# The order of 32 node tiles in two eight-head graph attention layers: from few edges to many, or few and many in turn

## The chip, the cores and the metric

The kernel runs on one core of one Trainium2 chip. The metric is the device time of one execution in microseconds (us), as a median of several runs.

## What is computed

The reference takes 4096 nodes with 512 features each (x) and a sparse 0/1 matrix adj. The chance of an edge between nodes i and j falls as 1/sqrt((i+1)(j+1)), so node 0 has many neighbours and node 4095 few. It runs two blocks, cut here to what matters:

```python
# block 0: eight heads of 64
h = einsum('nf,kfp->knp', x, W)
e = leaky_relu(f2[:, :, None] + f1[:, None, :])        # one score for each pair and head
att = softmax(where(adj > 0, e, -1e16), axis=-1)
x = layernorm(x + concat_heads(einsum('knm,kmp->knp', att, h)))
# block 1: eight heads of 64, then one head of 512, then two dense layers
h = elu(gat_heads(x, mask, W1, a1))
out = elu(gat_heads(h, mask, Wo, ao))
out = relu(out @ lin1_w + lin1_b) @ lin2_w + lin2_b
x = layernorm(x + out)
```

## The kernel before

The nodes are cut into 32 tiles of 128, tile 0 with the first 128 nodes. A first stage, `find_edges`, reads adj and writes a list of edges for each tile, in chunks of 128 edges: for each edge of a chunk the neighbour's number (`idx`) and the node's place in the tile (`nl`). How many chunks a tile has is fixed when the program is built, by the statistics of adj: 51 for tile 0, 21 for tile 1, 16, 14 and 13 for tiles 2 to 4, 11 for 5 and 6, 10 for 7, 9 for 8 to 10, 8 for 11 to 13, 7 for 14 to 19, 6 for 20 to 28 and 5 for 29 to 31. That is 309 chunks. `units_of` (line 1049) joins the chunks of a tile to units of at most 6: 11 units for tile 0, 4 for tile 1, 3 each for 2 to 4, 2 each for 5 to 19 and 1 each for 20 to 31. That is 66 units.

The two eight-head layers are two calls of `heads_layer` (line 1270); a third layer with one head and the dense layers follows and is written out below it with an order of its own. Each layer works from a table in HBM, one row for each node (its projected features and its score as a neighbour), and one row more, the mean of all, for nodes without edges. The first gather of a layer waits until the whole table of that layer stands.

What a layer does with a unit, in the class `Attention`:

- `gather` (line 1076): one indirect DMA for each chunk, issued by POOL, brings 128 rows of the table to a buffer g. The pool has `GB` = 7 buffers, each for one unit; the gather of unit i + 7 is issued after unit i and waits until PE has done with unit i's buffer.
- `spread` (lines 1094 to 1129), once for a tile: PE spreads the nodes' own scores to the edges (pss, lines 1101 and 1108), in cuts of at most 20 chunks; DVE collects each cut (line 1117) and makes ls (1129). There is one pss buffer. Where a tile has more than one cut, all but the last are collected at once, in the middle of DVE's queue.
- `weights` (1147 to 1155): DVE makes z of three small operations, ACT takes two exponentials, one of them (wp) to a single PSUM buffer.
- `add` (1179 to 1212): DVE makes the 0/1 matrices sm (1179) and multiplies the gathered rows by wp (1200); PE sums them over the edges into acc (1212), which has two buffers, each for one tile.

The order of all this is written out by hand in `heads_layer`. Its list `order` is 31, 30, ... 0, few edges first. Before the loop stand the gathers of the first 7 units, the spreads of the first two tiles and the weights of the first unit. One turn of the loop, for unit i, is: at a tile's first unit the spread of the tile two places on and the fetch of its input rows; `project`; the weights of unit i + 1; `add` of unit i; the gather of unit i + 7; then `split`, `rows`, `norm`, and at a tile's first unit `divide` for the tile before. So in DVE's queue z of the next unit stands ahead of the multiply of this one. These five steps finish a tile, one step a turn: `divide` (1220, 1232, then residual and layer norm statistics in the first layer, 1393 to 1259, or the elu in the second, 1247 and 1248), `norm` (1263 to 1266, or 1249, then a transpose on PE, 683, copied out by ACT, 686), `project` (697, into the next layer's features), `rows` (710 to 717, ACT copies them and SP writes them to the next layer's table), and `split` (723 to 733). A spread needs the result of `split` for its tile. It is made for 8 tiles at once, when the last of them is there; in the order 31 to 0 that is the tile that 8 divides.

After the last unit the mean row is finished (768 to 770) and written. In the first layer ACT clears the 7 buffers with one operation each before they are first used.

Of the kernel before, what the change touches and what calls it, by code (L numbers as in the profile page):

```python
# [24 lines left out]
NT = N // P  # L25
# [533 lines left out]
def sparse_path(  # L559
# [119 lines left out]
    def turn_in(sb, ps, st, src, t):  # L679

        pt = ps.tile([P, FC, P], F32, name="pt", tag="ph")
        for c in range(FC):
            nc.tensor.transpose(pt[:, c, :], src[:, ts(c, P)], ident)  # L683
        xt = sb.tile([P, FC, P], F32, name="xt")
        for c in range(FC):
            nc.scalar.activation(  # L686
                xt[:, c, :], pt[:, c, :], AF.Copy, accum_out=st.xparts[:, c, t : t + 1]
            )
        return xt

    def project_in(ps, st, columns, n=P):

        halves = []
        for j in range(2):
            ph = ps.tile([P, st.wide], F32, name="ph")
            for c in range(FC):
                nc.tensor.matmul(ph[:n], columns(c), st.w[:, c, j], start=(c == 0), stop=(c == FC - 1))  # L697
            halves.append(ph)
        return halves

    def project_out(sb, st, halves, t, n=P):

        hs = st.heads
        hrow = sb.tile([P, F + HS], F32, name="hrow")[:n, : st.row]
        if hs == 1:
            nc.scalar.copy(hrow[:, 0:1], ones[:n])
        for j, ph in enumerate(halves):
            part = HF + hs // 2 if hs > 1 else HF + j
            at = j * st.part if hs > 1 else 1 + j * HF
            nc.scalar.copy(hrow[:, at : at + part], ph[:n, :part])  # L710
        nc.sync.dma_start(st.table[t * P : t * P + n, :], hrow)
        st.hrow = hrow
        if t < NT:
            for j, ph in enumerate(halves):
                m = hs // 2 if hs > 1 else 1 - j
                if m:
                    nc.scalar.copy(st.s[:, t, j * m : (j + 1) * m], ph[:, st.wide - m :])

    def split_s(sb, st, lo, n):

        shape = [P, n, 2, st.heads]
        s2 = sb.tile([P, 8, 2, HS], F32, name="s2")[:, :n, :, : st.heads]
        nc.vector.tensor_tensor(
            s2,
            st.s[:, lo : lo + n, None, :].to_broadcast(shape),
            half[:, None, :, None].to_broadcast(shape),
            op=OP.mult,
        )
        part = st.s3[:, lo : lo + n]
        nc.vector.tensor_copy(part[:, :, :, 0, :], s2)  # L730
        nc.vector.tensor_sub(s2, s2, part[:, :, :, 0, :])
        nc.vector.tensor_copy(part[:, :, :, 1, :], s2)
        nc.vector.tensor_sub(part[:, :, :, 2, :], s2, part[:, :, :, 1, :])
# [8 lines left out]
    def mean_of_all_but(pool, ps, st, t):  # L742

        rest = pool.tile([P, 2, FC], F32, name="rest_mean")
        for i, (lo, hi) in enumerate(((0, t), (t + 1, NT))):
            if lo < hi:
                nc.vector.tensor_reduce(rest[:, i], st.xparts[:, :, lo:hi], AX.X, OP.add)
            else:
                nc.vector.memset(rest[:, i], 0.0)
        nc.vector.tensor_add(rest[:, 0], rest[:, 0], rest[:, 1])  # L750
        nc.vector.tensor_scalar_mul(rest[:, 0], rest[:, 0], 1.0 / N)
        halves = project_in(ps, st, lambda c: rest[:, 0, c : c + 1], 1)
        mrow = pool.tile([1, F + HS], F32, name="mrow")[:, : st.row]
        if st.heads == 1:
            nc.scalar.copy(mrow[:, 0:1], ones[:1])
        for j, ph in enumerate(halves):
            part = HF + st.heads // 2 if st.heads > 1 else HF + j
            at = j * st.part if st.heads > 1 else 1 + j * HF
            nc.scalar.copy(mrow[:, at : at + part], ph[:1, :part])
        return mrow  # L760
# [288 lines left out]
    def units_of(order):  # L1049
        units = []  # L1050
        for t in order:
            own = [
                Unit(t, [(p.first + i, n) for i, n in runs], slots)
                for p in pts if p.t == t for runs, *slots in p.units()
            ]
            own[0].first = own[-1].last = True
            units += own
        return units
# [211 lines left out]
    def heads_layer(gp, wk, sb, pp, st, nxt, fetch, finish, clear):  # L1270

        order = list(range(NT - 1, -1, -1))
        units = units_of(order)
        with tc.tile_pool(name=f"ha_{st.name}", bufs=2, space=PSUM, reuse_waits="tile") as pacc, \
                tc.tile_pool(name=f"hp_{st.name}", bufs=1, space=PSUM, reuse_waits="tile") as one, \
                tc.tile_pool(name=f"hq_{st.name}", bufs=2, space=PSUM, reuse_waits="tile") as ps, \
                tc.manual_schedule():  # L1280
            at = Attention(st, gp, wk, pacc, one)
            extra = {}
            if clear:
                for _ in range(GB):
                    g = gp.tile([P, GC * (F + HS)], F32, name="g")
                    nc.scalar.activation(g, ones.to_broadcast(g.shape), AF.Copy, scale=0.0)
            for u in units[:GB]:
                at.gather(u)
            for t in order[:2]:
                at.spread(t)()  # L1290
                extra[t] = fetch(t)
            at.weights(units[0])

            def divide(t):
                at.inverse(sb, t)
                o = at.normal(sb, t)
                return norm, t, o, finish(o, t, extra.pop(t))

            def norm(t, o, rest):
                rest()
                xt = turn_in(pp, ps, nxt, o, t)
                return project, t, xt

            def project(t, xt):
                return rows, t, project_in(ps, nxt, lambda c: xt[:, c, :])

            def rows(t, halves):
                project_out(pp, nxt, halves, t)  # L1310
                return (split, t) if t % 8 == 0 else None

            def split(t):
                split_s(pp, nxt, t, 8)

            def run(of):
                for way in list(ways):
                    if way[0] is of:
                        ways.remove(way)
                        nxt_ = of(*way[1:])  # L1320
                        if nxt_:
                            ways.append(nxt_)

            ways = []
            for i, u in enumerate(units):
                pos = order.index(u.t)
                spread = None
                if u.first and pos + 2 < NT:
                    spread = at.spread(order[pos + 2])
                    extra[order[pos + 2]] = fetch(order[pos + 2])  # L1330
                run(project)
                if i + 1 < len(units):
                    at.weights(units[i + 1])
                if i == len(units) - 1:
                    mrow = mean_of_all_but(pp, ps, nxt, u.t)
                at.add(u)
                if i + GB < len(units):
                    at.gather(units[i + GB])
                run(split)
                run(rows)  # L1340
                run(norm)
                if u.first and pos > 0:
                    ways.append((divide, order[pos - 1]))
                    run(divide)
                if spread:
                    spread()
            ways.append((divide, order[-1]))
            while ways:
                for of in (project, split, rows, norm, divide):
                    run(of)  # L1350
            finish_mean(ps, nxt, mrow)
# [4 lines left out]
    with ExitStack() as pools:  # L1356
# [6 lines left out]
        pp = pools.enter_context(tc.tile_pool(name="eq", bufs=2, space=PSUM))  # L1363
# [20 lines left out]
    pp = layers.enter_context(tc.tile_pool(name="lp", bufs=2, side="right", reuse_waits="tile"))  # L1384
# [7 lines left out]
    def finish0(o, t, xr):  # L1392
# [7 lines left out]
        return rest  # L1400

    heads_layer(gp, wk, sb, pp, st0, st1, fetch0, finish0, True)
    heads_layer(gp, wk, sb, pp, st1, st2, lambda t: None, lambda o, t, _: elu(sb, o), False)


    layers.close()
    with tc.tile_pool(name="tg", bufs=GT, side="right", reuse_waits="tile") as gp, \
# [12 lines left out]
        order = [t for block in blocks for t in block]  # L1420
# [176 lines left out]
```

## Time and profile before

| | us |
|---|---|
| median of 3 runs | 2143.87 (2143.78 to 2149.99) |
| the profiled execution's own time | 2328.89 |
| its span, first to last instruction | 2326.7 |
| first gather of the two eight-head layers and of the one-head layer | 499.7, 1031.7, 1556.5 |
| last L1200 multiply of the two eight-head layers ends | 1006.5, 1527.3 |
| mean granted TensorE clock | 0.885 of full |

| engine | busy us | share of the span |
|---|---|---|
| PE (matrix products) | 1776.6 | 76% |
| DVE (vector engine) | 1328.1 | 57% |
| POOL (issues the gathers) | 1161.8 | 50% |
| ACT (scalar engine) | 658.9 | 28% |

The profiled execution is 185.0 us longer than the median run, and 2.2 us of it lie around its span. A line of the timeline has start and duration in us, the engine, the line of the program, the operation, what it writes and reads, how many of it, and in brackets how long its engine was idle before it and what ended the idle time. A line of waits has the waiting operation, what it waited for, the total in us, how many times, and the longest. A line of a stretch has its bounds, its length, the busy time of PE, PE's weight loads, DVE, ACT and POOL with the number of instructions, the granted clock, the busy share of the DMA engines, and GB/s.

### The profile page before, as it was taken

Reading aid. Unit: us, or ns where it says so; the run is one execution under the profiler, and the core shown is the slowest. Engines: PE = TensorE matmul, PEld = TensorE weight load, DVE = VectorE, ACT = ScalarE, POOL = GpSimd, SP = SyncE. Lnnn points to the kernel's source line nnn. Section 1 sums busy time; section 2 is a strip of 40 time slices with the busy share of each in tenths; the row PEclk is TensorE's granted clock in tenths of the full one; section 3 lists DMA queues with packets and bytes.
Section 4 is the critical chain, followed back from the end, with each engine's and each line's share of the span. In section 5 each row is a group of like instructions: output and inputs, shape, how many; then the busy total and the mean of one; then the engine's idle time right before and its main releaser. Section 6 shows DMA issues by size and latency. Waiting matters only on the chain.

```text
span 2326.7 us, 29282 instructions
## 1 busy us (share of the span) xinstructions
PE 1776.6 (76%) x8987; PEld 1038.4 (45%) x8987; DVE 1328.1 (57%) x3920; ACT 658.9 (28%) x2311; POOL 1161.8 (50%) x1662
## 2 busy tenths in 40 slices
PE   4778776643987775754997767746999898998997
PEld 3555442212665543531665444424445444444444
DVE  6887776744998776733777655733243424334322
ACT  3446776650332211100433221101111111121121
POOL 5424444456556664627556665646355634444300
PEclk9989997866999896875999988877999999999999
DMA  6434665525667775625566665545354524335301
GB/s 222 141 115 159 224 256 207 210 80 163 201 209 219 212 209 144 174 60 145 154 159 170 175 182 145 158 128 143 87 150 131 170 81 148 101 110 151 93 16 52
DMA packets 132589, 351.94 MB, mean 151 GB/s; under 512 B 41922, under 2 KB 42954, under 8 KB 128454
## 3 DMA queue, kind: packets, MB, share of 16 engines
q0 software_dynamic: 74160, 206.25, 33.1%
q1 hardware_dynamic: 58262, 143.72, 17.5%
q8 instruction: 74, 1.21, 0.2%
q14 instruction: 93, 0.76, 0.1%
HBM read 347.31 MB, written 42.24 MB: 167 GB/s over the span
## 4 chain that ended last, share of the span: by engine, by line
PE 36%; DVE 12%; issue 9%; another core or an unknown queue 6%; DMA 3%; POOL 3%; ACT 2%; SPq 0%; DVEq 0%; POOLq 0%; ACTq 0%
PE acc L1212 13%; PE p L1475 9%; PE ph L697 6%; PE p L1487 5%; DVE g L1200 4%; POOL g L1076 3%; DMA g<-table_t,idx 2%; DMA xr<-sx_d 1%; PE pt L683 1%; DVE bs L1253 1%; DVE sm L1179 1%; DVE sm L1187 1%; DVE xr L1492 1%; DVE z L1147 1%
## 5 line engine op out<-in xcount | busy, mean ns | idle before, releaser
L1076 POOL DMA_INDIRECT g<-table_t,idx x927 | 937.4, 1011 | 720.1 <-PE acc L1212 352.9
L1212 PE MATMUL acc<-g,sm 128*64 128x260 f32 (+2 forms) x4068 | 619.9, 424 | 219.9 <-DVE g L1200 100.7
L1212 PEld LDWEIGHTS acc<-g,sm 128*64 128x64 f32 x4068 | 347.9, 150 | 462.7 <-issue 177.8
L697 PE MATMUL ph<-sw_t,xt 128*128 128x264 f32 (+1 forms) x1536 | 408.4, 415 | 82.1 <-ACT xt L686 46.3
L697 PEld LDWEIGHTS ph<-sw_t,xt 128*128 128x128 f32 x1536 | 303.4, 204 | 154.2 <-ACT xt L686 63.0
L1200 DVE TENSOR_TENSOR g<-g,wp 128x2048 f32<-128x2048 f32 (+3 forms) x132 | 349.1, 2645 | 22.8 <-ACT wp L1155 20.2
L884 DVE MAX8 cand<-key 128x8 f32<-128x353 f32 (+55 forms) x467 | 197.3, 449 | 77.7 <-PE key L878 77.1
L1475 PE MATMUL p<-sht,sl1w 128*128 128x512 f32 (+1 forms) x576 | 229.3, 553 | 2.2 <-issue 1.2
L1487 PE MATMUL p<-sl2w,shid 128*128 128x512 f32 x512 | 227.0, 598 | 0.0
L686 ACT ACTIVATE xt<-pt 128x128 f32<-128x128 f32 x384 | 101.1, 278 | 286.5 <-PE pt L683 132.3
L710 ACT COPY hrow<-ph 128x260 f32<-128x260 f32 (+2 forms) x194 | 71.1, 373 | 311.1 <-PE ph L697 146.2
L1475 PEld LDWEIGHTS p<-sht,sl1w 128*128 128x128 f32 x576 | 107.6, 191 | 114.0 <-issue 108.7
L1487 PEld LDWEIGHTS p<-sl2w,shid 128*128 128x128 f32 x512 | 95.4, 190 | 120.1 <-issue 119.3
L1249 DVE SCALAR_TENSOR_TENSOR o<-ex,o 128x512 f32<-128x512 f32 x64 | 44.4, 694 | 182.8 <-ACT ex L1248 145.1
L877 PE MATMUL key<-sg,s_identb 128*128 128x512 bf16 (+1 forms) x258 | 111.6, 434 | 15.4 <-DVE cand L884 10.1
L848 ACT ACTIVATE sg<-raw 128x4096 bf16<-128x4096 int32 (+1 forms) x39 | 116.9, 2998 | 6.6 <-DMA raw<-in_adj_dram 3.7
L1478 ACT ACTIVATE shid<-p,sl1b 128x512 f32<-128x512 f32 (+1 forms) x72 | 46.0, 639 | 249.5 <-PE p L1475 212.0
L878 PE MATMUL key<-frac,places 128*128 128x512 bf16 (+1 forms) x258 | 111.1, 431 | 2.7 <-POOL places L784 2.7
L1187 DVE TENSOR_SCALAR sm<-iota_n,nl,w 128x64 f32<-128x64 f32 x339 | 83.1, 328 | 31.9 <-ACT w L1158 31.1
L1147 DVE TENSOR_TENSOR z<-s,g 128x16 f32<-128x16 f32 (+9 forms) x291 | 43.6, 174 | 92.0 <-DMA g<-table_t,idx 83.7
L1117 DVE TENSOR_REDUCE s<-pss 128x48 f32<-128x144 f32 (+21 forms) x108 | 32.1, 298 | 102.3 <-remote 55.1
L686 ACT ACTIVATION_READ_ACCUMULATOR xt<-pt 128x1 f32 x384 | 79.7, 208 | 0.0
(185 smaller groups left out, 1811.3 us busy)
## 6 DMA issues: line engine op xcount, KB each, us to landing
raw<-in_adj_dram SPq DMA_DIRECT2D x31, 2048.0 KB
table_t<-hrow SPq DMA_DIRECT2D x64, 260.0 KB
xr<-in_x_dram SPq DMA_DIRECT2D x64, 256.0 KB
g<-table_t,idx POOLq DMA_INDIRECT x927
table_t<-hrow SPq DMA_DIRECT2D x32, 257.0 KB
sx_d<-o SPq DMA_DIRECT2D x32, 256.0 KB
xr<-sx_d SPq DMA_DIRECT2D x32, 256.0 KB
out_dram<-xr SPq DMA_DIRECT2D x32, 256.0 KB
```

Source lines behind the costliest of these rows:

```text
L686: nc.scalar.activation(xt[:, c, :], pt[:, c, :], AF.Copy, accum_out=st.xparts[:, c, t : t + 1])
L697: nc.tensor.matmul(ph[:n], columns(c), st.w[:, c, j], start=(c == 0), stop=(c == FC - 1))
L848: nc.scalar.activation(sg[:, ts(i, w)], raw[:, ts(i, w)], AF.Sign)
L877: nc.tensor.matmul(out_, ident_b, sg[:, j:e], start=True, stop=False)
L878: nc.tensor.matmul(out_, places[:, w], frac[:, j - w * KW : e - w * KW], start=False, stop=True)
L884: nc.vector.max(out=cand[:, at : at + 8], in_=part)
L1076: nc.gpsimd.indirect_dma_start(out=u.g[:, k, : self.st.row], out_offset=None, in_=self.st.table[:, :], in_offset=bass.IndirectOffsetOnAxis ...
L1187: nc.vector.tensor_scalar(sm[:, at + i], of_g, node[k], u.w[:, k], op0=OP.is_equal, op1=OP.mult)
L1200: nc.vector.tensor_mul(body, body, wp[:, :, :, None].to_broadcast(body.shape))
L1212: nc.tensor.matmul(out_[g * HN : (g + 1) * HN], sm[:, slot], rows(k), start=start, stop=stop)
L1475: nc.tensor.matmul(p1, l1w[:, c, ts(k, P)], hts[b][:, c, :n], start=(c == 0), stop=(c == FC - 1))
L1487: nc.tensor.matmul(p2, hids[b][:, k, ts(j, P)], l2w[:, k, :], start=(k == 0), stop=(k == HC - 1))
```

## The change

The list `order` is made anew in both eight-head layers: 31, 1, 30, 15, 29, 2, 28, 14, 27, 3, 26, 13, 25, 4, 24, 12, 23, 5, 22, 11, 21, 6, 20, 10, 19, 7, 18, 9, 17, 8, 16, 0. Tile 31 is still first and tile 0 last. Because groups of 8 tiles no longer end with the tile that 8 divides, `rows` keeps a set of the tiles that are out, and calls for the split of a group when all 8 are in it. Nothing else differs; the third layer keeps its order.

```diff
-        order = list(range(NT - 1, -1, -1))
+        many = [t for i in range(8) for t in (1 + i, NT // 2 - 1 - i)][: NT // 2 - 1]
+        order = [t for pair in zip(range(NT - 1, NT // 2, -1), many) for t in pair] + [NT // 2, 0]
+        assert sorted(order) == list(range(NT))
...
             def rows(t, halves):
                 project_out(pp, nxt, halves, t)
-                return (split, t) if t % 8 == 0 else None
-
-            def split(t):
-                split_s(pp, nxt, t, 8)
+                out_.add(t)
+                lo = t // 8 * 8
+                return (split, lo) if out_.issuperset(range(lo, lo + 8)) else None
+
+            def split(lo):
+                split_s(pp, nxt, lo, 8)
...
-            ways = []
+            ways, out_ = [], set()
```

## The prediction

> **What bounds the kernel now.** I read the page first, then the waits of each engine, then the timeline by tile. I call the two eight-head layers A (first gather at 499.7 us) and B (1031.7 us); the one-head layer's gathers begin at 1556.5 us. One layer gathers 309 chunks (927 over three layers) in 66 units (132 L1200 multiplies in A and B).
>
> ```profile
> L1076 POOL DMA_INDIRECT g<-table_t,idx x927 | 937.4, 1011 | 720.1 <-PE acc L1212 352.9
> ```
>
> The page's costliest group is the gather on POOL: 937.4 us of work, and 720.1 us of idle before it, half of that for a buffer which PE's acc has yet to free. So it is both the largest job and one that is often held up. The timeline at the start of B gives POOL's pitch and when a unit can be used:
>
> ```profile
> 1031.74 1.00 POOL L1076 DMA_INDIRECT g<-table_t,idx  x1 [39.65 <-DMA table_t<-mrow]
> 1033.04 0.99 POOL L1076 DMA_INDIRECT g<-table_t,idx  x1 [0.30 <-issue]
> ...
> 1036.95 1.00 POOL L1076 DMA_INDIRECT g<-table_t,idx  x1 [0.30 <-issue]
> ...
> 1040.59 0.20 DVE L1147 TENSOR_TENSOR z<-s,g 128x40 f32<-128x40 f32 x1 [10.86 <-DMA g<-table_t,idx]
> ```
>
> One gather every 1.30 us, so 309 x 1.304 = 402.9 us a layer if POOL never stands. The fifth chunk is issued by 1037.95 and DVE starts on it at 1040.59: 2.6 us to land.
>
> Next, stretches of the layers (us, then busy PE, PEld, DVE, ACT, POOL). Counting L1200 multiplies, the first line is tiles 24 to 20 of A, the second tiles 18 to 15, the third tile 0; then tiles 24 to 20 and tile 0 of B.
>
> ```profile
> 601.00:644.40 43.40, 41.21 (x268) 29.28 (x266) 41.12 (x89) 13.71 (x80) 20.08 (x20) 1.00 0.66 191
> 659.90:701.00 41.10, 34.28 (x231) 23.22 (x229) 38.28 (x100) 11.82 (x70) 26.91 (x26) 1.00 0.74 223
> 951.30:1006.50 55.20, 45.63 (x262) 27.84 (x260) 43.44 (x89) 7.03 (x39) 28.23 (x29) 0.88 0.46 128
> ```
> ```profile
> 1129.60:1169.70 40.10, 38.28 (x258) 27.71 (x259) 32.20 (x59) 17.25 (x85) 19.05 (x19) 1.00 0.50 138
> 1469.90:1527.30 57.40, 46.09 (x264) 28.13 (x263) 41.30 (x82) 8.14 (x40) 32.68 (x31) 0.91 0.47 127
> ```
>
> In A a tile of 6 chunks takes 43.40 / 5 = 8.68 us with DVE full, against 6 x 1.304 = 7.8 us of POOL: the consumers are behind. Tile 0 takes DVE 43.4 us of work against 51 x 1.304 = 66.5 us of POOL: POOL is behind, and lives on up to 7 units gathered ahead. In B the same tiles take 8.02 us (PE full) and 41.3 us of DVE. So the two regimes are real.
>
> Is time lost by their order? That needs a correction: the profiled execution is 2328.89 us against the median of 2143.87, 185.0 us more. PE's waits in A (first fence) and B (second) say where:
>
> ```profile
> PE acc L1212 <- issue: 27.8, 25, 2.9
> PE pss L1101 <- issue: 14.0, 2, 13.3
> PE ph L697 <- issue: 7.1, 11, 1.6
> ```
> ```profile
> PE acc L1212 <- issue: 43.7, 44, 7.0
> PE ph L697 <- issue: 22.9, 11, 13.6
> PE pss L1101 <- issue: 7.7, 2, 4.9
> ```
>
> "issue" is idle time for which the profile shows no cause; at 1068 to 1090 us PE starts single matmuls about 0.7 us apart. Sums: A 50.4 us with 1.5 of pss L1108, plus 21.3 of DVE "rd L1220 <- remote" at tiles 29 and 28; B 82.0 with pt L683 (5.7) and pss L1108 (2.0); the rest of the program 28.1. Together 181.8, close to 185.0: I take them as the tracing's own (an inference) and leave them out.
>
> A then lasts 1031.7 - 499.7 - 71.7 = 460.3 us, B 1556.5 - 1031.7 - 82.0 = 442.8. POOL's floor is 402.9, plus 6.6 from the last gather to the end of the last multiply (2.6 landing, 1.1 of z and exp, 2.8 multiply), plus the tail to the next layer's first gather (25.2 in A from 1006.5, 29.2 in B from 1527.3): 434.7 and 438.7. **A is 25.6 us over the floor, B 4.1.** That is all that an order can win: 29.7 us.
>
> [...]
>
> **The change part by part.** Instructions of every engine stay the same in number and size; POOL's 309 gathers per layer change only in which chunk they fetch. Only order moves.
>
> (1) Spread of tile 1 (21 chunks, two cuts, so DVE waits for PE in the middle of its queue) goes from tile 3's first unit to before the layer's first unit. In A DVE stood from 859.83 until PE's record ends at 865.7: 5.9 us removed. At the new place it is hidden under the wait for the first gather: in B the split of tiles 0 to 7, on which it now depends, ends at 1029.1 us and its two collects (0.66 and 0.17 us) have until 1040.6. If that cover were gone it would cost about 2 us. Spread of tile 0 (four cuts) goes from tile 2 to tile 8: same cost at either place, 0.
>
> (2) Tile 1 comes second, when POOL has no lead. A unit's multiply stands behind the next unit's z (L1147) in DVE's queue, so tile 1's last multiply needs 31 gathers: 31 x 1.304 + 2.6 + 1.1 + 1.8 = 45.9 us after the first gather. Unstarved it would be there at 16.8 (first multiply, 516.5 - 499.7) + 2.8 + 20.1 (tile 1's 25.9 us of period less 5.8 of idle) = 39.7: starved 6.2. Before, the first tiles starve 2.1 (DVE z <- DMA g). Cost 4.1 us. Queued behind that z on DVE are the multiply, norm and divide; nobody else waits long. Tile 1's own idle of 5.8 us lies inside the starved time, of which I count 3.5 (the wait of rd for PE) as gained.
>
> (3) POOL's lead before tile 0. By then DVE in A has done the pairs 31,1 to 17,8 and 16; POOL too, at nearly equal sums (pair 30,15: 8.68 + 41.10 / 4 = 19.0 against 12 x 1.304 = 15.6 us; pair 29,2: 8.68 + 18.3, tile 2's period less its idle, = 27.0 against 21 x 1.304 = 27.4). Lead at tile 0 is some units, as before. 0; bounds: A falls to its floor (-25.6), or the pairs leave A where it is.
>
> (4) SP: fetches, table and sx_d writes go with their tiles, same count. The layer's last row written is still tile 0's and then the mean, so the next layer's first gather waits for the same thing. 0. Splits of three groups come late (tiles 16, 8, 0) instead of spread: 5 small DVE operations each, 1.5 us, moved only.
>
> Sum for A: -5.9 + 4.1 - 3.5 = -5.3. For B, where POOL is within 4.1 us of being the bound, the same edits can give between 0 and -4.1; I take -1. Total -6: 2143.9 - 6 = **2138 us** (profiled about 2323). That is 0.27%, and 0.3% (6.4 us) is about what a measurement of this kernel can tell from no change.
>
> **Rivals.** *Full interleave:* with every pair near balance, A and B both end on POOL's floor: 2143.9 - 29.7 = 2114. For it: DVE's busy time from 516 to 1007 us is 366 us, under POOL's 403. Against: A's other 52 us (460.3 - 25.2 - 16.8 - 366) are waits inside units, which the order hardly touches.
>
> *Exposed finishing (slower):* the finishing of a tile runs through ACT and is hidden only in long units. In A and B:
>
> ```profile
> DVE rstd L1263 <- ACT rstd L1259: 21.6, 10, 5.3
> ```
> ```profile
> DVE o L1249 <- ACT ex L1248: 33.3, 14, 6.0
> ```
>
> But for 4.4 us at tile 26, A's part is in the 16 tiles 19 to 4, of two and three short units; tiles 25 to 20 show 0.2 us of idle each. Alternated, the 12 single-unit tiles are finished inside short units too. With the smaller rows of L1263, 26.4 - 4.4 = 22.0 us over 16 tiles is 1.4 us each; 12 more tiles cost 16.5 us in A, and B is covered by POOL. Then 2138 + 16.5 = 2154. It decides if these waits are real and not the echo of PE's unexplained waits, and if A's consumers, not POOL, end last; above 6 us it ends slower.
>
> *Nothing moves:* (1) and (2) cancel and POOL's blocked time was all tracing: 2144.
>
> **How the numbers follow.** Forecast 0.40 (2130 to 2144), full interleave 0.17, exposed finishing 0.25, nothing 0.18. Faster: half of the forecast and the interleave, 0.37. Same: half the forecast, most of the last, a little of the third, 0.37. Slower: 0.26. Range 2120 to 2158: it cuts the lower half of the interleave and the upper tail of the exposed finishing. The forecast's own range is 2130 to 2144.
>
> **What would show it.** In the changed profile: (1) no wait of some 20 us at L1117 in mid-layer; (2) waits of L1147 for g at tile 1's units, some 6 us a layer; (3) POOL's wait for acc in A far below 69.8 us if the interleave holds; the rival shows as L1263 and L1249 waiting on ACT more often than 10 and 14 times. I am wrong if PE's unexplained waits are real work, since then both layers are bound by the consumers throughout, or if a split or spread at a new place stops PE.

## The result and the profile after

| kernel | us, median | runs | ratio to before, 95% interval |
|---|---|---|---|
| before | 2143.82 (2140.20 to 2149.99) | 8 | |
| after | 2136.68 (2131.30 to 2139.29) | 8 | 0.9974 [0.9964, 0.9985] |

The change makes the kernel 0.26% faster, 5.6 us by the ratio, near the forecast of 2138. (The medians differ by 7.1 us; the recorded ratio lies closer to 1, and gains are taken from it here unless medians are named.) The number came out. Most of the steps that led to it did not, as the rest shows.

The first profile of before (2328.89 us) was taken where PE was slowed far more than in the runs of after in this table (granted clock 0.885, against 0.914 to 0.921), so I compare the profile of after (0.918) with a second profile of before (2146.02 us, 0.915, called *before again*).

The line that answers to the first one of the prediction, from the page of after:

```profile
L1076 POOL DMA_INDIRECT g<-table_t,idx x927 | 937.8, 1012 | 535.9 <-issue 229.1
```

The gathers cost POOL the same 1.01 us each, but the idle time before them fell from 720.1 to 535.9 us, and a buffer that PE has yet to free is no longer what ends most of it. The timeline at the start of B, in after:

```profile
944.12 1.00 POOL L1076 DMA_INDIRECT g<-table_t,idx  x1 [36.00 <-DVE ls L1129]
945.42 0.99 POOL L1076 DMA_INDIRECT g<-table_t,idx  x1 [0.30 <-issue]
...
949.32 1.00 POOL L1076 DMA_INDIRECT g<-table_t,idx  x1 [0.30 <-issue]
...
953.15 0.20 DVE L1147 TENSOR_TENSOR z<-s,g 128x40 f32<-128x40 f32 x1 [9.64 <-DMA g<-table_t,idx]
```

The pitch is 1.30 us, as before, and the first unit is usable 2.8 us after its last gather was issued. The release that is named for the first gather is a DVE operation, which ended at 943.51 us. But the gather starts 0.86 us after a DMA that landed at 943.26, and in before again, where the mean row's write (table_t) is the release named, it also starts 0.86 us after the landing (952.45 after 951.59); so I take that write to be what it waits for here too.

Whole layers, A then B: first for before again, then for after (columns as in the prediction: bounds, length, PE, PEld, DVE, ACT, POOL, clock, DMA share, GB/s).

```profile
505.05:952.45 447.40, 348.80 (x2234) 230.33 (x2234) 370.91 (x840) 116.37 (x588) 313.04 (x309) 0.91 0.71 210
952.45:1395.44 442.99, 344.13 (x2235) 229.55 (x2235) 313.55 (x648) 123.34 (x583) 324.64 (x314) 0.90 0.67 186
```
```profile
500.50:944.10 443.60, 353.81 (x2234) 232.60 (x2234) 372.52 (x840) 116.83 (x588) 313.69 (x309) 0.90 0.71 212
944.10:1384.10 440.00, 342.81 (x2224) 227.27 (x2224) 313.91 (x647) 123.65 (x583) 321.71 (x313) 0.92 0.69 188
```

Read the second column. A went from 447.4 to 443.6, B from 443.0 to 440.0, with the same work on every engine. POOL is "busy" for 313 us only, since the 0.30 us between two gathers are not counted; from its first gather to the end of its last it is 408 us. So a layer is best cut into three pieces that follow one another: POOL's gathers (with the time in which POOL is *held up*, that is, its idle over 0.30 us before a gather, counted where it is over 0.6), the *lag* from the end of the last gather to the end of the last multiply, and the *tail* from there to the next layer's first gather. The waits of POOL in A show what changed, before again and then after (waiting operation, what for, total us, times, longest):

```profile
POOL g L1076 <- PE acc L1212: 8.8, 7, 2.4
```
```profile
POOL g L1076 <- PE acc L1212: 1.2, 4, 0.3
```

Before, POOL stood in A seven times for a buffer, 8.8 us, of which 7 x 0.30 are the usual pause; after, the four waits are nothing but usual pauses. In the timeline of before again, five waits are longer than 0.6 us. Four of them, 5.0 of the 6.4 us beyond the usual pauses, lie at tiles 15 to 13, just after tiles 31 to 16; the second, in tile 15, is the first pair of lines here. The fifth lies in tile 0, near the end of A, in the second pair:

```profile
639.46 1.00 POOL L1076 DMA_INDIRECT g<-table_t,idx  x1 [0.30 <-issue]
642.33 0.99 POOL L1076 DMA_INDIRECT g<-table_t,idx  x1 [1.87 <-PE acc L1212]
...
904.65 1.00 POOL L1076 DMA_INDIRECT g<-table_t,idx  x1 [0.30 <-issue]
907.42 1.00 POOL L1076 DMA_INDIRECT g<-table_t,idx  x1 [1.78 <-PE acc L1212]
```

### The profile page after: what moved, and what is told of

Read it like the earlier page. It is cut to its first block, busy times and chain, and to the rows that moved or that the text cites. A ratio compares the mean times of both kernels' runs of the same rounds, so it can differ in the third digit from the quotient of the medians.

```text
span 2136.3 us, 29277 instructions
## 1 busy us (share of the span) xinstructions
PE 1721.8 (81%) x8987; PEld 1004.8 (47%) x8987; DVE 1328.6 (62%) x3920; ACT 663.4 (31%) x2311; POOL 1162.0 (54%) x1662
## 4 chain that ended last, share of the span: by engine, by line
PE 33%; DVE 17%; issue 16%; POOL 15%; DMA 12%; ACT 6%; SPq 0%; POOLq 0%; DVEq 0%; ACTq 0%
POOL g L1076 10%; DMA g<-table_t,idx 10%; PE acc L1212 10%; PE p L1479 9%; PE ph L697 6%; DVE g L1200 4%; PE p L1491 4%; DVE cand L884 2%; POOL s L944 1%; ACT sides L943 1%; DMA xr<-sx_d 1%; DVE cand L901 1%; DVE sm L1179 1%; DVE lst L899 1%; PE pl L967 1%
## 5 line engine op out<-in xcount | busy, mean ns | idle before, releaser
L1076 POOL DMA_INDIRECT g<-table_t,idx x927 | 937.8, 1012 | 535.9 <-issue 229.1
L1212 PE MATMUL acc<-g,sm 128*64 128x260 f32 (+2 forms) x4068 | 581.0, 416 | 182.7 <-DVE g L1200 141.6
L1212 PEld LDWEIGHTS acc<-g,sm 128*64 128x64 f32 x4068 | 327.9, 148 | 402.1 <-DVE g L1200 159.5
L697 PE MATMUL ph<-sw_t,xt 128*128 128x264 f32 (+1 forms) x1536 | 399.5, 409 | 54.3 <-ACT xt L686 47.8
L697 PEld LDWEIGHTS ph<-sw_t,xt 128*128 128x128 f32 x1536 | 296.5, 199 | 126.3 <-ACT xt L686 70.6
L1147 DVE TENSOR_TENSOR z<-s,g 128x16 f32<-128x16 f32 (+8 forms) x291 | 46.6, 175 | 162.7 <-DMA g<-table_t,idx 161.6
L1249 DVE SCALAR_TENSOR_TENSOR o<-ex,o 128x512 f32<-128x512 f32 x64 | 44.2, 691 | 122.0 <-ACT ex L1248 121.8
L1155 ACT ACTIVATE wp<-z 128x32 f32<-128x32 f32 (+3 forms) x132 | 27.2, 206 | 211.2 <-DVE g L1200 211.2
L1496 DVE TENSOR_TENSOR xr<-p,xr 128x512 f32<-128x512 f32 x32 | 22.0, 689 | 93.6 <-PE p L1491 93.2
```

Of the source, the lines that this page charges most:

```text
L1076: nc.gpsimd.indirect_dma_start(out=u.g[:, k, : self.st.row], out_offset=None, in_=self.st.table[:, :], in_offset=bass.IndirectOffsetOnAxis ...
L1212: nc.tensor.matmul(out_[g * HN : (g + 1) * HN], sm[:, slot], rows(k), start=start, stop=stop)
```

## The experiments

Times of a group are set beside before's runs on the same chip: 2141.04 us (e1 to e4), 2140.95 (e5 to e8), 2317.62 (e9 to e11) and 2142.01 (e12). The pieces of each profile are in this table, in us; the profile of before again is e1. "Rest" is from the third layer's first gather to the end of the last DVE operation (L1266), some 6 us before the span ends.

| run | order in A | A: gathers (held up) + lag + tail | A | order in B | B: gathers (held up) + lag + tail | B | rest |
|---|---|---|---|---|---|---|---|
| e1 | old | 413.8 (6.4) + 10.8 + 22.8 | 447.4 | old | 407.8 (0) + 8.4 + 26.8 | 443.0 | 742.3 |
| after | new | 407.6 (0) + 12.8 + 23.2 | 443.6 | new | 404.9 (0) + 8.3 + 26.8 | 440.0 | 746.0 |
| e12, after again | new | 408.4 (0) + 9.7 + 22.3 | 440.4 | new | 404.6 (0) + 8.4 + 26.7 | 439.7 | 742.0 |
| e2 | new | 408.5 (0) + 9.7 + 22.3 | 440.5 | old | 406.3 (0) + 8.3 + 27.8 | 442.4 | 746.5 |
| e3 | old | 415.2 (7.8) + 10.8 + 24.4 | 450.4 | new | 405.8 (0) + 8.3 + 26.5 | 440.6 | 740.9 |
| e4 | tile 1 second | 413.9 (5.6) + 10.8 + 22.7 | 447.4 | tile 1 second | 406.2 (0) + 8.3 + 27.8 | 442.4 | 746.4 |
| e5, 5 buffers | old | 425.7 (18.5) + 9.0 + 22.8 | 457.6 | old | 415.1 (8.0) + 8.3 + 29.3 | 452.8 | 742.7 |
| e6, 5 buffers | new | 418.5 (11.3) + 8.6 + 23.8 | 450.9 | new | 405.4 (0) + 8.3 + 28.3 | 442.0 | 742.3 |
| e7, 7 more gathers | new | 417.1 (0) + 8.4 + 22.0 | 447.6 | new | 415.7 (0) + 8.3 + 28.1 | 452.1 | 749.6 |
| e8 | tile 1 late | 408.9 (0) + 10.5 + 23.7 | 443.1 | tile 1 late | 405.9 (0) + 8.3 + 26.5 | 440.7 | 741.6 |

**e1: before again.** No edit.

> The kernel before, unchanged, once more, for a second profile of it and as a measure of the timing's own scatter: ratio 1.000 within 0.1%. If the 182 us of PE's waits without a cause in its first profile were the tracing's own, this profile may lack them, and its span is then near 2141 us. What the theories expect of its two eight-head layers (first gather to next first gather; in the changed kernel they measure 443.6 and 440.6 us, both with POOL never held up for a buffer): the prediction's split (the gain of some 5 us sits in layer A, the spread of tile 1 and the wait before tile 0) gives A about 449 and B about 441 to 442; the rival split (B, where the last tile's lead was short) gives A about 444 and B about 446. In either case POOL's waits for acc are the place where the excess over 443.6 and 440.6 shows.

Ratio 1.0002 [0.9992, 1.0011]. The new profile lacks the 182 us of PE's waits, though it was traced like the first, and places the excess in A, where POOL is held up.

**e2 and e3: the new order in one layer only.**

```diff
+        if st is not st0:
+            order = list(range(NT - 1, -1, -1))
         assert sorted(order) == list(range(NT))
```

(e3 has `if st is st0`.)

> The alternating order in the first eight-head layer (A) only; B keeps 31 to 0. The prediction's theory (nearly all in A): 5 to 5.5 us less than before, about 2138.5. The rival (the gain sits in B): within 1 us of before, about 2143.5. If the two layers share it evenly: about 2141.

> The alternating order in the second eight-head layer (B) only; A keeps 31 to 0. The prediction's theory: 1 us less than before or nothing, about 2143. The rival (the gain sits in B): 5 us less, about 2138.5. The two single-layer gains should add up to that of the whole change, 7 us in the runs (2136.7 against 2143.8), since nothing of one layer's order reaches the other.

A only: 2138.08, 0.9984 [0.9973, 0.9996], 3.4 us less. B only: 2142.38, 1.0001 [0.9992, 1.0010], nothing. By the timed runs the gain sits in A. The two sum to 3.2 us, and the whole change has 5.6 (interval 3.2 to 7.7); the intervals meet, no more can be said. The profiles have A shorter by 7.4 us in the mean (448.9 in e1 and e3, 441.5 in after, e2 and e12) and B by 2.6 (442.7 in e1 and e2, 440.1 in after, e3 and e12), more than the times do. One order's A scatters by 3 us between profiles and the rest of the program by 6, so single profiles give the place, and the timed runs the size.

**e4: tile 1 second, nothing else.**

```diff
+        order = [NT - 1, 1] + list(range(NT - 2, 1, -1)) + [0]
```

> One part of the change alone, in both layers: tile 1 is taken second, and everything else stays from few to many edges (31, 1, 30, 29, ... 2, 0). The theory of the prediction's step 1 and 2 (the two-cut spread of tile 1 in mid-layer is what is gained, the starved start is what is paid, the interleaving itself gives nothing): as fast as the whole change, 5 to 7 us less than before. The rival (the gain comes from POOL no longer being held up by full buffers, since small and large tiles alternate): within 2 us of before, and POOL's wait for acc stays in the profile as in the kernel before.

2141.55, 1.0003 [0.9995, 1.0011]: nothing, as the rival said. Yet the wait that it was to remove did go. DVE's waits for spreads in A, before again and e4:

```profile
DVE s L1117 <- PE pss L1108: 13.5, 4, 7.0
```
```profile
POOL g L1076 <- PE acc L1212: 8.0, 7, 1.9
...
DVE s L1117 <- PE pss L1108: 6.7, 4, 5.2
```

6.8 us of DVE's waiting are gone, POOL is still held up (5.6 us), and A lasts 447.4 us as before, with the same gathers and the same lag. So in this order the wait of 7.0 us at that place cost the layer nothing that the profile shows. e4 adds tile 1's early start while it removes the wait, so the timed run shows only that the two together give nothing. A longer wait there may reach the path: in e3's profile it is 9.4 us, and POOL is held up in tile 0 for 3.7 us in place of 1.5; no run settles this.

**e5 and e6: five gather buffers in place of seven, old order and new.**

```diff
-GB = 7
+GB = 5
```

> The order of before with 5 gather buffers in place of 7. In the second profile of before, POOL is held up for full buffers in layer A only (6.4 us in all, at tiles 15 to 13 and in tile 0), and its lead of 7 units is spent in tile 0. Theory (POOL is the bound of both layers, and the order decides how long it is held up): with two buffers fewer POOL is held up earlier in A and enters tile 0 with two units less in hand, each some 5 chunks of 1.304 us, so A grows by about 13 us less the 2.5 us by which its consumers now end behind POOL: 10 us; B, whose lead is 2 to 3 units, by 0 to 2. Total 2151 to 2153, ratio 1.005. Rival (the gain of the change comes from the spread of tile 1, or is chance, and the buffers have no part in it): within 3 us of before.

> The alternating order with 5 gather buffers in place of 7. Theory (POOL is the bound; alternation keeps the consumers' lag behind POOL small until the last pairs): POOL is held up a little in A, by 1 or 2 units near tiles 9, 8 and 16, of which the 4.5 us by which A's consumers end behind POOL hides most; A +1 to +5 us against the alternating order with 7, B 0. So 2134 to 2141 beside before, and the distance from the old order with 5 buffers grows from 6 to some 12 us. Rival (buffers have no part): the distance between the two orders stays at 6 us.

Old order 2161.82, 1.0088 [1.0070, 1.0106]; new order 2141.86, 1.0002 [0.9992, 1.0012]. The distance between the orders is 20 us where it was 6. I had expected 12, and both times came out above their ranges: I took B to have buffers to spare with five, and in the old order it is held up too (B 452.8, 9.8 us more than in e1); in the new order A grew by 7 to 10 us where 1 to 5 were expected. POOL's waits in A and in B of e5:

```profile
POOL g L1076 <- PE acc L1212: 22.5, 13, 5.1
```
```profile
POOL g L1076 <- PE acc L1212: 10.1, 7, 3.1
```

and in A and B of e6:

```profile
POOL g L1076 <- PE acc L1212: 14.3, 10, 2.2
```
```profile
POOL g L1076 <- PE acc L1212: 1.0, 3, 0.4
```

What alternation saves is buffers. With few of them it is worth much, with seven little, because seven nearly suffice for the old order.

**e7: more gathers for POOL, in the new order.**

```diff
+            if self.st.heads > 1 and len(u.chunks) == 3:
+                nc.gpsimd.indirect_dma_start(
+                    out=u.g[:, 3, : self.st.row],
...
```

> The alternating order, and one more gather (of a chunk that is there already, into the free part of the buffer, read by nobody) in each unit of three chunks of the two eight-head layers: 7 units, 7 x 1.304 = 9.1 us of POOL a layer, 18.3 us in all, and nothing more on DVE, PE or ACT. Theory (POOL is the bound of both layers, never held up): nearly all of it is seen, B by 9.1 us, A by 9.1 us less the 4.5 us by which its consumers end behind POOL, at least 4.6: 14 to 18 us more than the alternating order, 2150 to 2155. Rival (DVE or the consumers' waits set A and B): 0 to 6 us more, 2136 to 2143.

2155.32, 1.0059 [1.0041, 1.0076], against 0.9974 without the gathers: 0.0085, or 18 us (19 against e12, the change on the same chip), for 18.3 us of gathers. By the intervals about 4 us either way are open, but nearly all of it is seen. A pays 9 us in gathers and gets some back as lag (8.4 in place of 9.7 to 12.8), as expected; B's gathers grow by 10.8. POOL's stream of gathers is the bound of both layers in the new order. Each added gather also moves its rows by DMA, so e7 alone doesn't part POOL's issuing from the transfers; that it is the issuing is argued from the even pitch of 1.30 us.

**e8: tile 1 next to last.**

```diff
+        order = [t for t in order if t != 1][:-1] + [1, 0]
```

> The alternating order with tile 1 taken out of the second place and put just ahead of tile 0 (31, 30, 15, 29, 2, 28, 14, ... 8, 16, 1, 0). The prediction's steps 1 and 2 (the spread of tile 1 in mid-layer costs 5.9 us in A, tile 1's starved start 4.1 less 3.5 us of its idle that is gained): some 5 us slower than the alternating order, no faster than before. The POOL theory (neither of them counts, only POOL's held-up time and the consumers' lag at the end): POOL is not held up, tile 1 ahead of tile 0 takes POOL 27 us and the consumers 24, so the lag at the end of A falls from 12.8 towards 9.7 us, and A and B end as in the alternating order or up to 3 us earlier: 2133 to 2137.

2134.67, 0.9964 [0.9953, 0.9976]. The spread of tile 1 is back in mid-layer and its starved start gone, and neither is felt; as in e4, the two go together. By the ratios it is 2.1 us less than the change, or 1.3 beside e12, with intervals that overlap: not shown to be better.

**e9, e10, e11.**

e9 searched for a better order, e10 is the changed kernel once more, e11 is the old order with the edit of e7:

```diff
+        order = [31, 30, 29, 28, 15, 27, 2, 26, 14, 25, 3, 24, 13, 23, 4, 22,
+                 12, 21, 5, 20, 11, 19, 6, 18, 10, 17, 7, 16, 9, 8, 1, 0]
```

> A search for a better order, by the POOL theory: four tiles of few edges first (31 to 28), so that the consumers waste less time waiting for gathers at the start; then large and small in turn (15, 27, 2, 26, 14, 25, 3, ... 9, 8), and tiles 1 and 0 last. If POOL is not held up, A and B end on POOL's time (407.5 and 405.5 us of gathers) plus a lag of 8.3 to 10 us and the tails of 22.5 and 26.8: A 438 to 441, B 440 to 441, so 0 to 4 us less than with tile 1 late, 2131 to 2135. If the early small tiles fill the 7 buffers in A, POOL is held up by a few us and it is no better than the alternating order: 2136 to 2140.

> The changed kernel once more, unchanged, for a second profile of it and a second measure beside before: ratio 0.996 to 0.9985 as before. A 440 to 444 us, B 440 to 441, POOL not held up in either, lag at the end of A 10 to 13 us. It also shows by how much the unchanged third layer and what follows scatter (741 to 747 us in the profiles so far).

> The order of before with the same 7 more gathers a layer as were added to the alternating order (where they cost 18.6 us, 2155.3 against 2136.7). POOL theory: POOL's held-up time in A lies at tiles 15 to 13 and in tile 0, just behind six of the added gathers, and takes part of their time, about 5 of 9.1 us; in B, where POOL is never held up, 9.1 to 11 are seen. So A + 4 to 6, B + 9 to 11: 13 to 17 us more than before, 2154 to 2158, and the two orders come within 3 us of each other. Rival (POOL's held-up time is not what separates the orders): as many us as in the alternating order, 18 to 19 more, 2159 to 2160.

All three expectations missed, since on this chip everything took some 180 us longer: before 2317.62 (2310.55 to 2329.95, 30 runs), e9 2328.75, 1.0042 [1.0029, 1.0056], e10 2335.05, 1.0071 [1.0043, 1.0099], e11 2332.90, 1.0064 [1.0041, 1.0086]. Here the change is *slower*, by 16 us. The questions of e9 and e11 stay unanswered, as they were asked of a PE without these pauses. What differs, the page's row of PE's granted clock shows (tenths, 40 slices), for the first profile of before, for e10, and for after:

```profile
PEclk9989997866999896875999988877999999999999
```
```profile
PEclk9889997767878899877788899887999999999999
```
```profile
PEclk8999998786999999878999999889999999999999
```

Between 500 and 1570 us the records of the clock add up to 340 us at half clock in the first profile of before, 333 in e9, 304 in e11 and 348 in e10, against 198 in before again, 195 in after and 164 in e12. And PE is slower in such a stretch than the granted clock tells. A stretch of before's first profile, one of e10 and one of after, all at half clock:

```profile
1063.00:1096.00 33.00, 13.07 (x28) 4.50 (x29) 3.96 (x4) 0.21 (x1) 24.41 (x25) 0.50 0.56 151
```
```profile
1062.00:1085.00 23.00, 5.91 (x14) 1.69 (x10) 4.52 (x12) 1.47 (x3) 14.83 (x16) 0.50 0.50 138
```
```profile
607.00:617.00 10.00, 9.03 (x30) 5.76 (x31) 9.48 (x30) 2.50 (x14) 7.87 (x8) 0.51 0.83 253
```

28 matrix products in 33 us and 14 in 23, against 30 in 10. These pauses are the waits without a cause. PE's waits of this kind that are over 0.5 us add up, in A and B together, to 121 us in the first profile of before, 100 in e9, 157 in e10 and 121 in e11, and to at most 4 us in every other profile. Those of e10 in layer A:

```profile
PE acc L1212 <- issue: 57.7, 19, 22.1
PE ph L697 <- issue: 7.4, 7, 1.9
PE pss L1101 <- issue: 6.0, 3, 3.0
PE pt L683 <- issue: 5.6, 2, 4.7
```

While PE pauses, the consumers are the bound and POOL waits in either order: held up for 86.4 and 76.2 us in A and B of before's first profile, 88.7 and 88.3 in those of e10. Alternation takes none of this away. But the consumers are not the bound throughout: e11's 18.3 us of added gathers cost about 15 us by the ratio (9.5 to 20), so POOL's time still counts between the pauses. Why the change loses 16 us I can't settle. e10 has only 8 us more at half clock than that profile of before, but 36 us more of PE's pauses in the two layers, and B of e10 has "o L1249 <- ACT ex" at 49.7 us (33.3 before), which is the exposed finishing of the rivals; but it is one profile of each, and the one of before may be of another chip.

**e12: the change once more.** No edit.

> The changed kernel a third time, unchanged, since its effect had two signs: 0.9974 of before where before took 2143.8 us, and 1.0071 where before took 2317.6 us and PE ran at half clock for longer. Theory (the sign goes with the state of PE: where it is little throttled, POOL is the bound and the alternation takes away POOL's held-up time; where it is throttled for some 320 us of the two layers, the consumers are the bound and the alternation has nothing to give): if before takes about 2141 us here, the ratio is 0.996 to 0.9985, A 440 to 444 and B 440 to 441 us with POOL never held up; if before takes about 2318, the ratio is 1.004 to 1.010, A and B near 530 and 535 us, with POOL held up for over 80 us in each. Rival (the second measure was chance): the ratio does not follow the time of before.

Before took 2142.01 us here, the change 2134.48 (2129.55 to 2142.28, 16 runs), 0.9970 [0.9959, 0.9980], with A and B at 440.4 and 439.7 and POOL never held up. So the gain is there in two measures where PE is little slowed (mean granted clock of the change's runs 0.918 and 0.920), the loss in one where it is slowed (0.882), and the sign went with the time of before. The clock alone doesn't make the gain: across the runs of one kernel here the time falls by about 0.9 us for each 0.001 of mean granted clock, and the change's runs have 0.9196 against 0.9172, so that some 2 us of the 6.6 between the means go with the clock; a straight line through both sets of runs leaves 4.5 us (an estimate, 3 to 6) at equal clock.

## Why the prediction was right, and where it was not

The forecast of 2138 was met at 2136.7, but by luck: the terms that made the sum gave nothing, and the gain came from one that was put at 0.

*The correction.* I took the 182 us of PE's waits for the tracing's own. That was wrong: before again was traced as well and has hardly any of them (3 us over 0.5 in the two layers), and before's 30 runs beside e9 to e11 took 2310.6 to 2330.0, so that its first profile (2328.89) lies among them. The granted clock of the stretch at 1063 to 1096 us, where I saw single matmuls 0.7 us apart, is 0.50; I had not looked at it there. In after, PE is busy for 29% (median; 59% at most) of the 3 us before each of 53 changes of its granted clock to 0.50, and for 82% or more before each of 52 changes back to 1.00. So the longer half clock can itself follow from the pauses, and is not shown to be their cause.

Subtracting the waits was right for B all the same (442.8, measured 442.4 and 443.0) and left A 10 to 13 us too long (460.3, measured 447.4 and 450.4). The sum for A was wrong in both directions: 12.5 of the 21.3 us of "rd L1220" fall on waits of PE that were already in the 50.4, while DVE's stand at L1117 up to 880.20, 14.5 us after PE's records end, stayed in but for the 5.9 of step 1, and so did 21.6 us at L1263 for ACT (0.6 in before again). That the 181.8 came close to 185.0 was chance. So "A is 25.6 us over the floor" was mis-sized: with 407.5 us of gathers (402.9 in the prediction, which took every gather at the usual pitch), 8.3 of lag (6.6 there) and 22.5 of tail the floor is 438.3, and A stood 9 to 12 over it.

*Step 1, the spread of tile 1, -5.9 and -3.5.* The wait was there and went (13.5 to 6.7 us in e4, 4.0 in after), and the time did not follow. The step failed because I added up DVE's waits in a layer in which POOL's stream is what ends last.

*Step 2, tile 1's starved start, +4.1.* Starved it is: 4.2 us at tile 1 in A of after and 6.0 in B, where 6 were forecast, and its last multiply ends 46.4 and 45.7 us after the layer's first gather, where 45.9 were forecast. It cost nothing that can be seen: in e4 and e8, which make and undo both moves, the layers are as long as without. The two errors of steps 1 and 2 have opposite signs; neither was tested without the other.

*Step 3, POOL's lead, 0.* This was the step that mattered. POOL's held-up time in A went from 6.4 and 7.8 us to 0, and A's gathers shortened by as much. I had compared the sums of pairs and looked at the lead before tile 0 alone, and called a difference of a few units none; four of the five waits of before again lie at tiles 15 to 13. The sums also took 8.68 us, the period of tiles of six chunks, for tiles 30 and 29, which have five.

*Step 4* held: the tails stay at 22 to 28 us.

*Full interleave* was the right mechanism: both layers now end on POOL's stream. It would give 2114 only if the 29.7 us had been there; 9 to 12 were. Of B's 2 us in the profiles I know only that its gathers take longer than 1.05 us less often (13 times, 13 and 16 in after, e12 and e3; 24 and 18 in e1 and e2); why is open.

*Exposed finishing* did not happen in the runs of the result: L1263 waits for ACT once in A, 0.6 us, and B's L1249 11.1 us in after against 10.3 in before again. The waits from which it was priced are nearly absent from before again too (0.6 us at L1263), so they went with PE's pauses, as its own condition had it. It may be part of the loss in e10.

*The condition* at the end of the prediction, wrong if PE's waits are real and both layers are bound by the consumers throughout, describes e10 in part: the forecast's sign fails there, but e11 speaks against "throughout".

## What to carry to other kernels

Interleaving light and heavy pieces saves buffers of the stream between two stages before it saves time: look for the producer's waits for a free buffer, and expect no more than their sum, here 6 to 8 us with seven buffers and 26 with five (of which 20 were won). A wait on an engine that is not the last one may be removed without any effect on the time; find first which stream ends the layer, by its first start, last end, and what follows. Before a profile is corrected for something that it doesn't explain, look at the clock beside it, and take a second profile.

## What was not expected of the hardware

The same kernel took 2141 us on two chips and 2318 on a third, and the change had the opposite sign there. The third was measured in one sitting, so the chip and the moment can't be told apart. PE's clock stood at half for 304 to 348 us between 500 and 1570 us in the four slow profiles, and for 164 to 208 us in the ten others. In half-clock stretches of the slow profiles, PE started 14 matrix products in 23 us and 28 in 33; elsewhere 30 in 10 us at the same granted clock. So the granted clock alone does not tell how fast PE runs; what holds it up in these stretches stays open.
